# Image/text attention: fourteen slots a group, second scores issued first, values one chunk a slot

## The chip, the cores and the metric

The kernel runs on one core of one Trainium2 chip. The metric is the device time of one execution in microseconds, as the median of the runs shown. The program is one launch that computes eight layers one after the other; the change touches one of them, the image/text attention.

## The reference, cut to what matters

The residual stream x has 4 batches of 256 tokens with 256 channels. The stage below adds an attention of these tokens to a context of 1601 positions a batch: the first 257 are image positions, the other 1344 text. Each kind has its own keys, values and softmax, and the two results are added.

```python
def _L2_xattn_ref(x, context, q_w, ...):          # NH = 16 heads of HD = 16
    ctx_img, ctx_txt = context[:, :257], context[:, 257:]
    q = rms_norm(linear(x, q_w, q_b), norm_q_w).reshape(B, L, NH, HD)
    k = rms_norm(linear(ctx_txt, k_w, k_b), norm_k_w)...      # text
    v = linear(ctx_txt, v_w, v_b)...
    k_img = rms_norm(linear(ctx_img, k_img_w, k_img_b), norm_k_img_w)...
    v_img = linear(ctx_img, v_img_w, v_img_b)...
    out = attention(q, k, v) + attention(q, k_img, v_img)     # softmax(q k / 4) v
    return linear(out, o_w, o_b)

x = x + _L2_xattn_ref(_layernorm(x), ctx_2048, ...)
```

## The kernel before, in words

The function `image_text` (from L1399) does this stage. The host has put the text positions first, so the context is 1344 text columns and then 257 image columns; in chunks of 128 that makes 13 chunks, of which chunk 10 (`mixed`) holds both kinds and chunk 12 has 65 columns. A group is one batch and four heads, so there are 16 groups, four a batch. A head's keys and queries lie on 32 partitions (16 channels, and two more columns that carry the two softmax shifts), so four heads fill the 128 rows of TensorE's array.

Each group is worked on three times:

- First scores, `maxima` (matmul L1572): queries stationary, keys streamed, for the maxima of text and image alone. VectorE reduces them (L1578 text, L1581 image with its sign turned, L1583 over the text pieces). A step takes one query tile of 128 (of two), one of four stretches in `SEGS` (512, 512, 320 and 257 columns) and two heads: 16 steps.
- Second scores, `weights` (L1618): keys stationary, the 256 queries streamed, one pair of chunks and two heads a step: 14 steps, the last two with one chunk. ScalarE takes the exponential into `pt` (L1624).
- Values, `values` (L1639): four heads' matmuls for each chunk, accumulated in one PSUM bank. The mixed chunk counts twice, so there are 14 sets.

All engines but SyncE follow an order written out by hand (`manual_schedule`). Time is cut into slots, `LEN` = 16 for a group. In a slot the loop at the end calls `maxima` for the next group and `weights` for this one, which issue their matmuls at once, and then runs the phases: early, mid (the reductions and exponentials just made), late, pe. Values of a whole pair of chunks come in the pe phase of every second slot from slot 3 on. Slots 14 and 15 have no second scores. First scores of a slot use one half of the array's rows and second scores the other half (`hp`), and the halves swap from slot to slot.

Both kinds of scores draw their PSUM buffer from one ring of three (`ps_sc`, two banks each). Projections, transposes and the output share a ring of one bank (`ps_tr`), and the accumulator is a ring of one (`ps_acc`).

The keys, values and queries of the next batch are produced meanwhile by `produce_keys` and `produce_queries`: a projection (L1527, L1483), one slot later the bias addition on VectorE (L1534, L1489), the square on ScalarE (L1464), the root (VectorE L121, then POOL's power L122), the value copy on POOL (L1538) and the scaling (L1542), then four transposes (L1550), and the copy out of PSUM by `evac`, which alternates between VectorE (L96) and ScalarE (L98). They are placed at `SLOTS` = (2, 5, 8, 11, 15) of three groups of the batch before, those of batch 0 in a prologue of 30 slots. The context comes by one DMA a batch from SyncE's queue (L177), into a single buffer. `finish` copies a group's accumulator (L1651), transposes it (L1656), divides by the sums (L1665 to L1670), and for a batch's last group adds the output projection (L1686, L1699) to x (L181).

Of the kernel before, what the change touches and what calls it, by code (L numbers as in the profile page):

```python
# [18 lines left out]
P = 128  # L19
# [33 lines left out]
def kernel(ctx: ExitStack, tc: tile.TileContext, A, out: bass.AP):  # L53
# [1345 lines left out]
    def image_text(xT):  # L1399
# [4 lines left out]
        half = TXT - mixed * P  # L1404
        G4 = NH2 // 4
        VW = HD2 + 1
        SEGS = [(0, 512), (512, 512), (1024, TXT - 1024), (TXT, IMG)]
        LEN = 16
        groups = [(b, g) for b in range(B) for g in range(G4)]
        ET = mybir.EngineType  # L1410
        with (
# [46 lines left out]
            def heads(ap):  # L1458
                return ap.rearrange("p (h d) -> p h d", h=NH2)

            def rms(src, n):
                sq = pool.tile([P, D], F32, tag="sq", name="sq", bufs=1)
                ss = small([P, 1], "ss1")
                nc.scalar.activation(sq[:n], src, AF.Square, accum_out=ss[:n])  # L1464
                rs = small([P, 1], "rs1")
                rsqrt(rs[:n], ss[:n], 1.0 / D, 1e-6, n, 1)
                return rs

            def fetch(b):
                state[b] = dict(  # L1470
                    ctxT=load_ctxT(b),
                    KT=pool.tile([P, G4, NCTX], F32, tag="KT", name="KT"),
                    QT=pool.tile([P, G4, S], F32, tag="QT0", name="QT0"),
                )

            def produce_queries(b, tt, t, bank):
                Q = qpads[b % 2]
                v = {}

                def project():  # L1480
                    v["ps"] = bank()
                    for c in range(NC_):
                        nc.tensor.matmul(  # L1483
                            v["ps"][:, :D], xtok(xT, b * 2 + tt, c), wq[:, c, :], start=(c == 0), stop=(c == NC_ - 1)
                        )

                def norm():
                    v["kb"] = pool.tile([P, D], F32, tag="kb", name="kb")
                    nc.vector.tensor_tensor(v["kb"], v["ps"][:, :D], qp[:, 0, :], ALU.add)  # L1489
                    v["rs"] = rms(v["kb"], P)  # L1490
                    nc.gpsimd.memset(Q[:, tt, :, HD2 : HD2 + 2], 0.0)

                def scale():
                    nc.vector.scalar_tensor_tensor(
                        Q[:, tt, :, 0:HD2], heads(v["kb"]), v["rs"], heads(qp[:, 1, :]), ALU.mult, ALU.mult
                    )

                def transpose():
                    v["tr"] = ps_tr().rearrange("p (g t) -> p g t", g=G4)
                    for g in range(G4):  # L1500
                        nc.tensor.transpose(
                            v["tr"][:, g, :], Q[:, tt, g * 4 : g * 4 + 4, :].rearrange("p h d -> p (h d)"), ident
                        )

                def out():
                    evac(state[b]["QT"][:, :, tt * P : (tt + 1) * P], v["tr"])

                begin(t, project, norm, scale, transpose, out)

            def begin(t, project, norm, scale, transpose, out):  # L1510
                at(t, "pe", project)
                at(t + 1, "early", norm)
                at(t + 1, "late", scale)
                at(t + 2, "pe", transpose)
                at(t + 3, "early", out)

            def produce_keys(b, k, t, bank):
                o, n = ch[k]
# [13 lines left out]
                def norm():  # L1532
                    v["kv"] = pool.tile([P, 2 * D], F32, tag="kv", name="kv")
                    nc.vector.tensor_tensor(v["kv"][:n], v["ps"][:n], kvp[:n, kind, 0 : 2 * D], ALU.add)  # L1534
                    v["rs"] = rms(v["kv"][:n, 0:D], n)
                    for lo, hi, place in [[(0, n, k)], [(0, half, k), (half, n, nch)], [(0, n, k)]][kind]:
                        vk = vbufs[b % 2][lo:hi, place, 0 : NH2 * VW].rearrange("p (h d) -> p h d", h=NH2)
                        nc.gpsimd.tensor_copy(vk[:, :, 0:HD2], heads(v["kv"][lo:hi, D : 2 * D]))  # L1538

                def scale():  # L1540
                    v["kp"] = kpads[(k % 2, 2, 3 + k % 2)[kind]]
# [11 lines left out]
                        )  # L1553

                def out():
                    evac(state[b]["KT"][:, :, o : o + n], v["tr"][:, :, :n])

                begin(t, project, norm, scale, transpose, out)

            def maxima(i, m):  # L1560

                b, g = groups[i]
                KT, QT, Q = state[b]["KT"], state[b]["QT"], qpads[b % 2]
                tt, s, hp = m // 8, m // 2 % 4, 1 - m % 2
                o, n = SEGS[s]
                if m % 8 == 0:
                    state["mx", tt] = small([P, 4, 3], f"mx{tt}", 2)
                mx = state["mx", tt]
                st = ps_sc()
                for j in range(2):  # L1570
                    r = slice(64 * hp + 32 * j, 64 * hp + 32 * j + 32)
                    nc.tensor.matmul(  # L1572
                        st[:, j, :n], QT[r, g, tt * P : (tt + 1) * P], KT[r, g, o : o + n], start=True, stop=True
                    )

                def rest():
                    if s < 3:
                        nc.vector.tensor_reduce(mx[:, 2 * hp : 2 * hp + 2, s], st[:, :, :n], AX.X, ALU.max)  # L1578
                    else:
                        h = g * 4 + 2 * hp  # L1580
                        nc.vector.tensor_reduce(Q[:, tt, h : h + 2, HD2 + 1], st[:, :, :n], AX.X, ALU.max, negate=True)  # L1581
                    if m % 8 == 7:
                        nc.vector.tensor_reduce(Q[:, tt, g * 4 : g * 4 + 4, HD2], mx, AX.X, ALU.max, negate=True)  # L1583

                return rest

            def queries(i, t):
# [11 lines left out]

                def out():  # L1600
                    state["QT", i] = pool.tile([P, S], F32, tag="QT1", name="QT1")
                    evac(state["QT", i], v["tr"][:, 0:S])

                at(t, "pe", transpose)
                at(t + 1, "early", out)
# [19 lines left out]

                return rest

            def values(i, c):
                b, g = groups[i]
                if c == 0:  # L1630
                    state["acc"] = ps_acc().rearrange("p (k t) -> p k t", k=2)
                acc, V, pt = state["acc"], vbufs[b % 2], state.pop(("pt", i, c))
                for q, (o, n) in enumerate(pairs[c]):
                    k = 2 * c + q
                    kind = (k >= mixed) + (k > mixed)
                    for a, place in [[(0, k)], [(0, k), (1, nch)], [(1, k)]][kind]:
                        for j in range(4):
                            h = g * 4 + j
                            nc.tensor.matmul(  # L1639
                                acc[32 * j : 32 * j + 32, a, :], V[:n, place, h * VW : h * VW + 32], pt[:n, j, q, :],  # L1640
                                start=(k == 0), stop=(k == nch - 1), skip_group_check=True,
                            )

            def finish(i, t):

# [27 lines left out]
                    )  # L1673

                at(t, "early", copy)
                at(t + 3, "pe", transpose)
                at(t + 4, "early", divide)
                if g < G4 - 1:
                    return

# [26 lines left out]
                        nc.gpsimd.tensor_tensor(X[j], X[j], qp[:, 2, :], ALU.add)  # L1707
                        residual(j, v["ps"][:, tt * D : (tt + 1) * D])

                at(t + 6, "pe", turn)  # L1710
                at(t + 7, "early", turned)
                at(t + 9, "pe", project)
                at(t + 10, "early", add)

            first = -30
            SLOTS = (2, 5, 8, 11, 15)
            for b in range(B):
                t0 = LEN * G4 * (b - 1) if b else first
                at(t0 - 2 if b else t0, "early", lambda b=b: fetch(b))
                for k in range(nch + 2):  # L1720
                    t = t0 + (k // 5 * LEN + SLOTS[k % 5] if b else k)
                    bank = (lambda: ps_sc()[:, 0, :]) if b == 0 else ps_tr
                    if k < 2:
                        produce_queries(b, k, t, bank)
                    else:
                        produce_keys(b, k - 2, t, bank)
            n = len(groups)
            for i in range(n):
                queries(i, LEN * i - 2)
                finish(i, LEN * (i + 1))  # L1730
            for t in range(first, LEN * n + 11):
                rest = []
                i, m = divmod(t + 2 + LEN, LEN)
                if 0 <= i < n:
                    rest.append(maxima(i, m))
                i, k = divmod(t, LEN)
                if 0 <= i < n:
                    if k < 2 * len(pairs):
                        rest.append(weights(i, k))
                    if k >= 3 and k % 2:  # L1740
                        at(t, "pe", lambda i=i, c=(k - 3) // 2: values(i, c))
                for phase in ("early", "mid", "late", "pe"):
                    for f in rest if phase == "mid" else todo.pop((t, phase), ()):
                        f()
            if todo:
# [616 lines left out]
```

## Time and profile before

| what | value |
| --- | --- |
| median of three runs | 3859.56 us (3857.51 to 3865.17) |
| the profiled execution | 3858.06 us |
| its span | 3856.3 us |
| TensorE busy in the span | 3603.5 us, 93% |
| VectorE, ScalarE, POOL busy | 2611.3, 1688.0, 1310.3 us |
| second scores L1618 | 1664 matmul passes, 235.7 us busy |
| first scores L1572 | 1024 matmul passes, 229.0 us busy |
| exponentials L1624 | 224, mean 960 ns |
| text reductions L1578 | 192, mean 1089 ns |

The profile is one execution. TensorE's rows count passes: an fp32 matmul appears as two passes, each with its own load of stationary weights (PEld). Lines of the timeline merge instructions of one group: start, length until the last of them ends, engine, line, operation, out and in, the count, and in brackets the idle time of that engine before, with what ended it. The chain of work is followed back from the last instruction; its lines give start, length and what ran. Ends of matmuls are modelled, so starts are the surer times.

### The profile page before, as it was taken

The numbers are of one execution on the slowest core, as the hardware profiler recorded it, in microseconds if no ns is written. First come the engines' busy times: TensorE is split into PE (matmuls) and PEld (weight loads), VectorE is DVE, ScalarE is ACT, GpSimd is POOL, SyncE is SP. The second block draws the span as 40 slices with busy tenths as digits, with TensorE's granted clock in tenths as the row PEclk, the third lists the DMA queues.
The fourth block names the chain that finished last, engine by engine and source line by source line (L and its number), as shares of the span: only waits on it lengthen the run. The fifth ranks groups of instructions, "written<-read, shape, count | busy, mean of one in ns | idle before, by whom it ended". The sixth has DMA issues, their size and how long they took to land.

```text
span 3856.3 us, 63026 instructions
## 1 busy us (share of the span) xinstructions
PE 3603.5 (93%) x23397; PEld 2157.0 (56%) x23397; DVE 2611.3 (68%) x5142; ACT 1688.0 (44%) x4956; POOL 1310.3 (34%) x2091
## 2 busy tenths in 40 slices
PE   8887969999999999999899999987999999999998
PEld 4556944555565555555544454553555556556655
DVE  7884857777777777777665655525767767667664
ACT  4443635444454544444134444422433444444432
POOL 2332534454454444544310101012333333333422
PEclk9987979999999999999989999988999999999999
DMA  7326342222122222220100000033111111211104
GB/s 241 100 67 238 79 150 60 65 71 72 55 60 66 65 81 55 56 54 8 56 18 18 1 18 1 1 132 130 41 55 42 55 32 38 55 38 37 30 3 132
DMA packets 173715, 248.50 MB, mean 64 GB/s; under 512 B 21581, under 2 KB 134881, under 8 KB 169825
## 3 DMA queue, kind: packets, MB, share of 16 engines
q1 hardware_dynamic: 167025, 233.00, 19.5%
q0 software_dynamic: 6384, 11.47, 1.4%
q8 instruction: 186, 3.05, 0.3%
q14 instruction: 120, 0.98, 0.1%
HBM read 199.39 MB, written 45.03 MB: 63 GB/s over the span
## 4 chain that ended last, share of the span: by engine, by line
PE 64%; DVE 18%; POOL 7%; issue 5%; ACT 3%; DMA 3%; SPq 1%; POOLq 0%; DVEq 0%; ACTq 0%
PE acc L1322 15%; PE sc L1242 13%; PE tr L1111 5%; PE sc L1618 4%; DVE PT L1296 4%; PE sc L1572 3%; PE tr L1185 3%; PE acc L1639 3%; POOL pe L1291 3%; PE acc L884 2%; PE tr L1527 2%; PE tr L1335 2%; POOL t L1158 2%; DVE ms L1250 2%; ACT pe L1251 2%
## 5 line engine op out<-in xcount | busy, mean ns | idle before, releaser
L1251 ACT ACTIVATE pe<-sc,ms 128x480 f32<-128x480 f32 (+1 forms) x1024 | 644.0, 632 | 940.2 <-DVE ms L1250 922.9
L1322 PE MATMUL acc<-PT,V 128*128 128x256 f32 (+1 forms) x3584 | 898.4, 391 | 7.7 <-ACT OT L1329 7.2
L1242 PE MATMUL sc<-KT,QT 128*32 128x480 f32 (+5 forms) x8192 | 887.7, 535 | 14.2 <-ACT pe L1251 6.3
L1291 POOL TENSOR_SCALAR pe<-pe,fac 128x480 f32<-128x480 f32 (+1 forms) x1024 | 655.3, 660 | 613.4 <-ACT pe L1251 282.3
L1322 PEld LDWEIGHTS acc<-PT,V 128*128 128x128 f32 (+1 forms) x3584 | 643.2, 190 | 352.2 <-issue 182.1
L1250 DVE TENSOR_REDUCE ms<-sc 128x1 f32<-128x480 f32 (+1 forms) x1024 | 607.5, 615 | 173.3 <-PE sc L1242 147.2
L1296 DVE STREAM_TRANSPOSE PT<-pe 128x1920 f32<-128x1920 f32 (+1 forms) x256 | 519.5, 2030 | 0.0
L122 POOL TENSOR_TENSOR rs<-rsq_t,mhalf 128x2 f32<-128x2 f32 (+2 forms) x248 | 160.1, 646 | 863.8 <-DVE rsq_t L121 804.7
L1242 PEld LDWEIGHTS sc<-KT,QT 128*32 128x32 f32 x8192 | 218.1, 109 | 408.1 <-issue 309.2
L1111 PE MATMUL tr<-w,cx 128*128 128x256 f32 (+1 forms) x1264 | 303.5, 382 | 1.3 <-ACT nk L1127 1.3
L1624 ACT ACTIVATE pt<-sc 128x1024 f32<-128x1024 f32 (+1 forms) x224 | 214.1, 960 | 201.2 <-PE sc L1618 192.9
L1578 DVE TENSOR_REDUCE mx<-sc 128x2 f32<-128x1024 f32 (+1 forms) x192 | 207.2, 1089 | 114.8 <-PE sc L1572 65.5
L1618 PE MATMUL sc<-QT,KT 32*128 32x256 f32 (+1 forms) x1664 | 235.7, 405 | 21.2 <-DVE mx L1578 14.5
L1111 PEld LDWEIGHTS tr<-w,cx 128*128 128x128 f32 (+1 forms) x1264 | 226.7, 187 | 31.6 <-ACT nk L1127 2.0
L1572 PE MATMUL sc<-KT,QT 32*128 32x512 f32 (+2 forms) x1024 | 229.0, 553 | 0.7 <-DVE mx L1578 0.7
L1251 ACT ACTIVATION_READ_ACCUMULATOR pe<-sc,ms 128x1 f32 x1024 | 199.9, 195 | 0.0
L1618 PEld LDWEIGHTS sc<-QT,KT 32*128 32x128 f32 (+1 forms) x1664 | 136.5, 182 | 79.1 <-DVE mx L1578 51.2
L122 POOL TENSOR_TENSOR rsq<-rsq_t,mhalf 128x4 f32<-128x4 f32 x64 | 65.0, 1016 | 326.4 <-DVE rsq_t L121 326.4
L1119 ACT ACTIVATE sq<-tr 128x128 f32<-128x128 f32 (+1 forms) x348 | 97.1, 279 | 169.2 <-PE tr L1111 162.7
L121 DVE TENSOR_SCALAR rsq_t<-ss 128x2 f32<-128x2 f32 (+2 forms) x248 | 45.7, 185 | 172.1 <-ACT sq L1119 134.8
L1185 PE MATMUL tr<-w,xlnT 128*128 128x512 f32 x256 | 126.1, 618 | 4.4 <-DMA w<-in_l1a_wkv 3.2
L1572 PEld LDWEIGHTS sc<-KT,QT 32*128 32x128 f32 x1024 | 84.3, 190 | 76.6 <-issue 42.2
(430 smaller groups left out, 4849.1 us busy)
## 6 DMA issues: line engine op xcount, KB each, us to landing
cx<-in_ctxT SPq DMA_DIRECT2D x144, 256.0 KB, 3.1
tab<-rope SPq DMA_DIRECT2D x112, 256.0 KB, 2.7
w<-in_l0f_w SPq DMA_DIRECT2D x8, 2048.0 KB, 17.0
ctxT<-in_ctxT SPq DMA_DIRECT2D x7, 1601.0 KB, 6.4
w<-in_l2f_w SPq DMA_DIRECT2D x8, 1088.0 KB, 15.6
w<-in_l1a_wq SPq DMA_DIRECT2D x16, 512.0 KB
wo<-in_l1a_wo SPq DMA_DIRECT2D x16, 512.0 KB, 6.4
w<-in_l3a_wq SPq DMA_DIRECT2D x16, 512.0 KB, 7.1
```

What stands on the lines that cost most here:

```text
L122: nc.gpsimd.tensor_tensor(dst, t[:n, :k], mhalf[:n, :k], ALU.pow)
L1111: nc.tensor.matmul(v["ps"][:n, i, :], lhs, st["wkv"][:, c, :], start=(c == 0), stop=(c == NC_ - 1))
L1185: nc.tensor.matmul(v["ps"], xtok(xT, b * 2 + tt, c), state[u]["wq"][:, c, :], start=(c == 0), stop=(c == NC_ - 1))
L1242: nc.tensor.matmul(sc[32 * r : 32 * r + 32, 0 : lens[r]], st["QT"][:, tt, o : o + 32], st["KT"][:, r, 0 : lens[r]], start=True, stop=True,)
L1250: nc.vector.tensor_reduce(top, sc, AX.X, ALU.max, negate=True)
L1251: nc.scalar.activation(w, sc, AF.Exp, bias=top, accum_out=s)
L1291: nc.gpsimd.tensor_scalar(w, w, v["fac"][:, g * 4 + a : g * 4 + a + 1], 1.0, ALU.mult, ALU.mult)
L1296: nc.vector.transpose(state[steps[i]][:, :, g * P : (g + 1) * P].rearrange("p k (a t) -> p a k t", a=4), pes[g].rearrange("p a (k i) -> p ...
L1322: nc.tensor.matmul(v["ps"][:, 0 : 2 * P], V[:n, k, :], PT[:n, k, :], start=(k == 0), stop=(k == nch - 1))
L1572: nc.tensor.matmul(st[:, j, :n], QT[r, g, tt * P : (tt + 1) * P], KT[r, g, o : o + n], start=True, stop=True)
L1618: nc.tensor.matmul(st[:n, j, q, :], KT[r, g, o : o + n], QT[r, :], start=True, stop=True)
L1624: nc.scalar.activation(pt[:n, 2 * hp : 2 * hp + 2, :m], st[:n, :, :m], AF.Exp)
```

## The change

- `LEN` becomes 14. `FIRST` replaces `SEGS`: first scores are made in seven stretches and two halves of heads. The first stretch is the image part of query tile 0 (257 columns); the text of tile 0 followed by text and image of tile 1 is cut into six stretches of 491 (the last 490) columns. One stretch holds the end of tile 0's text and the start of tile 1's, with two matmuls a head and two reductions; one holds text and image.
- In a slot `weights` is called ahead of `maxima`.
- `SETS` lists the 14 sets of values; one set runs in a phase of its own in each of slots 3 to 16, so the last three lie in the next group's slots. `finish` moves with it.
- In production the square, the root and the scaling are spread over two slots; the copies of keys and queries out of PSUM go to VectorE only from batch 1 on, and those of each group's queries always.
- Keys are placed at `SLOTS` over three groups, image chunks first; the queries of a batch lie in the last group of two batches before. The context is asked for four slots ahead of its batch's production instead of two. The prologue has 29 slots.

```diff
-        SEGS = [(0, 512), (512, 512), (1024, TXT - 1024), (TXT, IMG)]
-        LEN = 16
+        LEN = 14
+        step = -(-(TXT + NCTX) // (LEN // 2 - 1))
+        FIRST = [[(0, TXT, IMG)]]
+        for lo in range(0, TXT + NCTX, step):
+            hi = min(lo + step, TXT + NCTX)
+            cuts = [(0, lo, min(hi, TXT) - lo), (1, max(lo, TXT) - TXT, hi - max(lo, TXT))]
+            FIRST.append([c for c in cuts if c[2] > 0])
+        SETS = []
+        for k in range(nch):
+            SETS += [(k, 0, k), (k, 1, nch)] if k == mixed else [(k, int(k > mixed), k)]
...
-            def begin(t, project, norm, scale, transpose, out):
+            def begin(t, project, norm, square, root, scale, transpose, out):
                 at(t, "pe", project)
                 at(t + 1, "early", norm)
-                at(t + 1, "late", scale)
-                at(t + 2, "pe", transpose)
-                at(t + 3, "early", out)
+                at(t + 1, "late", square)
+                at(t + 2, "early", root)
+                at(t + 2, "late", scale)
+                at(t + 3, "pe", transpose)
+                at(t + 4, "early", out)
...
-                    evac(state[b]["KT"][:, :, o : o + n], v["tr"][:, :, :n])
+                    evac(state[b]["KT"][:, :, o : o + n], v["tr"][:, :, :n], "v" if b else "av")
...
             def maxima(i, m):
-                tt, s, hp = m // 8, m // 2 % 4, 1 - m % 2
+                s, hp = m // 2, 1 - m % 2
...
+                for tt, o, n in FIRST[s]:
+                    for j in range(2):
+                        r = slice(64 * hp + 32 * j, 64 * hp + 32 * j + 32)
+                        nc.tensor.matmul(
+                            st[:, j, c : c + n], QT[r, g, tt * P : (tt + 1) * P], KT[r, g, o : o + n],
+                            start=True, stop=True,
+                        )
...
-            def values(i, c):
+            def values(i, x):
+                k, a, place = SETS[x]
...
-                at(t + 3, "pe", transpose)
-                at(t + 4, "early", divide)
+                at(t + 1, "pe", transpose)
+                at(t + 2, "early", divide)
...
-            first = -30
-            SLOTS = (2, 5, 8, 11, 15)
+            SLOTS = (2, 6, 8, 10, 14, 16, 20, 22, 24, 28, 30, 34, 36)
+            ORDER = [*range(mixed, nch), *range(mixed)]
+            first = -29
...
+                tq = (t0 - LEN, t0 - LEN + 6) if b else (t0, t0 + 1)
+                at(t0 - 4 if b else t0, "early", lambda b=b: fetch(b))
+                for i, k in enumerate(ORDER):
+                    produce_keys(b, k, t0 + (SLOTS[i] if b else 2 + i), bank)
...
-                finish(i, LEN * (i + 1))
+                finish(i, LEN * (i + 1) + 3)
+                for x in range(len(SETS)):
+                    at(LEN * i + 3 + x, "values", lambda i=i, x=x: values(i, x))
...
+                if 0 <= i < n and k < 2 * len(pairs):
+                    rest.append(weights(i, k))
                 i, m = divmod(t + 2 + LEN, LEN)
                 if 0 <= i < n:
                     rest.append(maxima(i, m))
-                    if k >= 3 and k % 2:
-                        at(t, "pe", lambda i=i, c=(k - 3) // 2: values(i, c))
-                for phase in ("early", "mid", "late", "pe"):
+                for phase in ("early", "mid", "late", "values", "pe"):
```

## The prediction

> **What bounds the kernel now.** I read the chain of waits first, then the stretches, the waits, and the timeline of one group. The page has TensorE (PE) busy for 93% of the span. The image/text stage runs from about 1890 to 2533 us. These lines of its chain mark groups: the 24 values matmuls (x24, two passes for each fp32 matmul) are slot 15 of a group.
>
> ```profile
> 2438.14 1.92 PE tr L1699 x8
> ...
> 2446.94 1.43 PE acc L1639 x24
> ...
> 2468.32 1.24 DVE mx L1578
> 2469.60 1.13 PE sc L1618 x8
> ...
> 2477.61 1.43 PE acc L1639 x24
> ...
> 2508.28 1.43 PE acc L1639 x24
> ```
>
> A group that produces no keys takes 30.67 us (2446.94 to 2477.61 to 2508.28). Between its matmuls stands a VectorE (DVE) reduction: PE waits for it. The same marker in the busier batches stands at 1990.85, 2032.05, 2073.22, 2106.34 and 2145.22: 41.2 us for a group with five keys. Each of the first three batches takes 154.0 us (462 us from 1953.7, the first second score, to 2415.8).
>
> ```profile
> core 0: us, PE busy (x) PEld busy (x) DVE busy (x) ACT busy (x) POOL busy (x), PEclk, DMA share, GB/s
> ...
> 2261.00:2415.00 154.00, 148.71 (x1296) 77.29 (x1291) 92.54 (x150) 67.54 (x101) 18.68 (x38) 1.00 0.00 1
> 2415.00:2509.00 94.00, 89.01 (x878) 49.16 (x874) 51.61 (x73) 42.89 (x47) 0.00 (x0) 1.00 0.01 1
> ```
>
> DVE is busy 60% of a batch, ScalarE (ACT) 44%, POOL 12%; the granted clock is 1.00 and DMA idle. So the stage has no second full engine; it has PE work and PE waits. Where they lie, one pair of slots shows:
>
> ```profile
> 2462.62 0.70 PE L1572 MATMUL sc<-KT,QT 32*128 32x512 f32 x2
> 2462.64 0.70 PE L1618 MATMUL sc<-QT,KT 32*128 32x256 f32 x4
> 2463.16 0.59 PE L1572 MATMUL sc<-KT,QT 32*128 32x512 f32 x2
> 2463.17 0.60 PE L1618 MATMUL sc<-QT,KT 32*128 32x256 f32 x4
> 2463.60 1.02 PE L1572 MATMUL sc<-KT,QT 32*128 32x512 f32 x4
> 2463.80 2.36 DVE L1578 TENSOR_REDUCE mx<-sc 128x2 f32<-128x1024 f32 x2 [2.35 <-PE sc L1618]
> 2463.95 1.02 ACT L1624 ACTIVATE pt<-sc 128x1024 f32<-128x1024 f32 x1 [1.19 <-PE sc L1618]
> 2465.08 1.13 PE L1618 MATMUL sc<-QT,KT 32*128 32x256 f32 x8 [0.45 <-DVE mx L1578]
> 2466.14 1.07 PE L1639 MATMUL acc<-pt,vbuf 128*32 128x256 f32 x16
> 2467.14 0.70 PE L1572 MATMUL sc<-KT,QT 32*128 32x512 f32 x2
> ```
>
> First scores (L1572) and second scores (L1618) use opposite halves of the array's rows, so they start together. The next second scores need the buffer that DVE is reading: 2462.62 to 2465.08, 2.46 us, of which 0.96 is their work. The pair ends with second scores alone (1.06) and the values of two chunks (1.00): 4.52 us.
>
> **Durations used.** From those rows: a stretch of two passes streams 0.86 us (512 columns, or two times 256), plus 0.10 before it and 0.10 after it where the array's tiling changes. So scores of one slot 1.06, values of one chunk 0.10+0.43+0.10 = 0.63 (two chunks took 1.00). From the first second-score matmul to its exponential: 1.32 (2462.63 to 2463.95) or 1.18 (2465.08 to 2466.26), mean 1.25; exponential 1.02; to the matmul it releases 0.05 (2512.85 to 2512.90 in the last group).
>
> **The change, part by part.**
>
> *Order and ring.* With second scores first and three buffers, second scores reuse what first scores of two slots ago left: DVE has a full slot more and drops out. First scores reuse the buffer of the previous slot's second scores, so they wait for ACT: 1.25+1.02+0.05 = 2.32 us from second scores to the next first scores. Then come first scores (0.10 + 0.82 for 491 columns), 0.10 and values 0.63, 1.65 together. Two slots take 2.32+1.65 = 3.97, about 2.0 a slot, where PE's own work is 1.69. So each slot keeps a wait of 0.3 us, now for ACT. Behind the waiting first scores PE's queue holds the slot's values, transposes and the next second scores, and for those ACT waits in turn; the loop is therefore counted whole.
>
> *Fourteen slots and equal stretches.* First scores keep 3202 columns a group and half of rows and 32 matmuls, but lie in 12 slots of 491 columns beside 512 of second scores, and two of 257 beside 256. The two slots without second scores vanish. A group without keys: 12 x 2.0 = 24.0; two short slots of 0.63+0.63 and 0.15 wait, 2.8; the two query transposes 0.4 and the output's four 0.6 (four took 0.59, 2457.47 to 2458.06), 1.0, half of it inside the ACT wait: 27.3 us, against 30.67. Values of one chunk a slot double the tiling changes; that is in the 0.63. The cut at the end of a query tile adds two reductions a group, 2 x 0.09 us (1024 elements take 1.22, 640 take 0.82, so 0.10 is fixed), beside PE. Values' later slots only shift the end.
>
> *Production.* A key costs PE 1.91 (1.72 stream and changes) plus 0.62 for its transposes, 2.5; the 0.3 waits of the two slots it sits in hide 0.6: 1.9. Before it cost (41.2-30.67)/5 = 2.1. Its PSUM copy-outs move to DVE in later batches (0.69, before half on ACT at 0.58). DVE then does, per two slots with one key, 2 x 1.2 + 0.69 + 0.15 + 0.54 + 0.69 = 4.5 us, PE 2.5 + 3.4 = 5.9: hidden; without that cover it would cost some 0.7 a key. Squares (ACT 0.61) go behind the exponential, scaled roots a slot later, POOL's power (0.54) and value copy (0.40) with them; POOL is 12% busy, and nothing waits at its head. A batch: 4 x 27.3 + 13 x 1.9 + two queries 2.1 (projection 1.05 and transposes 0.6 each, less 0.6) + output projection 1.9 (turn 0.62, project 1.92, less 0.6) = 138. Against 154.0: -16 x 3 = -48.
>
> *Groups 12 to 14*: 3 x 27.3 + 1.9 = 83.8, before 93.9 (2414.35 to 2508.28): -10. *Group 15* has second scores and values only. Before, two slots' second scores ran side by side:
>
> ```profile
> 2512.90 1.13 PE L1618 MATMUL sc<-QT,KT 32*128 32x256 f32 x8 [0.32 <-ACT pt L1624]
> ...
> 2515.55 1.16 PE L1618 MATMUL sc<-QT,KT 32*128 32x256 f32 x16
> ```
>
> Now values stand between: 12 x 1.69 + 2 x 1.26 + 3 values slots at the end is 25 us, before some 18: +7. *Prologue*: key slots took 3.0 us (bias additions at 1907.58, 1910.28, 1913.58), a chain DVE 0.68, ACT 0.61, DVE 0.15, POOL 0.54, DVE 0.59 inside one slot. Split over two slots, PE's 2.5 binds: ten slots x 0.45, and one slot fewer: -6. *Moved loads*: the four context loads (SP queue, 6.4 us to land) are asked for at the latest four slots and 8 us ahead, with nothing else in SP's queue; the buffer is free 20 slots before. No cost; uncovered it would be 6 us each.
>
> **Sum**: -48 -10 +7 -6 = -57 us. The profiled execution took 3858.06 us (span 3856.3), 1.5 under the median 3859.56. 3858.06 - 57 = 3801, plus 1.5: 3802.5.
>
> **A rule against it.** The sum needs first scores to start beside second scores that stand ahead of them in PE's queue with eight passes. The row above shows it: 16 passes take 1.16 us, 8 take 1.13. The second eight belong to the other half of rows and come later in the program. The Trainium skill's "TensorE: Matmul & The Clock Gate", section "The mechanism", says that matmuls keep program order in start and end, and only weight loads go ahead. By it, first scores would start with the last second-score pass, 0.65 us late (0.10 + 3 x 0.215 = 0.75 in, less the 0.10 load): a slot 1.06 - 0.22 + 0.82 + 0.63 = 2.3. Then a group is 12 x 2.3 + 3.0 + 1.0 = 31.6, a batch 126.4 + 13 x 2.5 + 5.9 (queries and output unhidden) = 165, and the stage +33 +3 +7 -6 = +37. I take the row.
>
> **Rivals.**
> 1. *First scores start late* (slower). One mechanism, at PE's queue, priced by the rule: 3858 + 37 + 1.5 = 3897. With a delay d, 39 slots that follow a projection pay d, the other 141 pay d - 0.3: the gain of 57 is gone at d = 0.55. Against it: the last group, and the pair above, where second scores start 0.02 after first scores that have a pass outstanding. Chance 0.08.
> 2. *Smaller gain: a longer ACT or DVE loop.* ACT has copies and squares in its one queue; DVE, between 60% and 76% of a slot pair, may reach a reduction late. If each of 180 slots loses 0.15, -57 becomes -30: 3829. For it: the new wait is real. Against: ACT is 44% busy. Chance 0.11.
> 3. *Nothing moves*: another wait refills what is saved, 3860. The chain runs through these matmuls without a gap, so I give it 0.03.
>
> The forecast has 0.78, with 3789 to 3820: the ends are 0.07 us a slot less wait over 180 slots, and 0.1 more.
>
> **How the numbers follow.** What a measurement can tell from no change is about 0.2%, 8 us. Faster: 0.78 + 0.11 = 0.89; same 0.03; slower 0.08. The range 3789 to 3833 takes the forecast and most of rival 2.
>
> **What would show it.** Markers of groups without keys 27 us apart, of batches 138; first scores waiting for ACT exponentials 0.3 us, DVE waits at second scores gone; first and second scores starting within 0.03 us where neither waits; stage end near 2476. Wrong if first scores start after second scores end, if the x8 values rows are followed by gaps over 0.2, or if batches stay over 150.

## The result, and the profile after

The changed kernel takes **3791.88 us** (median of 6 runs, 3789.63 to 3795.2) against 3859.03 for the kernel before (6 runs beside it). The ratio is 0.9824, with a 95% interval of 0.9811 to 0.9836. The forecast was 3802.5, so the sign, the path and the place were right, and the gain of 67 us is 10 us more than predicted. The profiled execution took 3789.63 us, its span is 3787.9: 68.4 less than before.

The page's first line gives the shares. TensorE (PE) is now busy for 94% of the span instead of 93%, with 44 us less busy time for the same 23397 instructions. In a batch, at a granted clock of 1.00 in both, it is busy for 136.89 us instead of 148.71, because more of them lie side by side.

```profile
PE 3559.4 (94%) x23397; PEld 2124.8 (56%) x23397; DVE 2623.3 (69%) x5204; ACT 1675.6 (44%) x4926; POOL 1315.1 (35%) x2091
```

The stretches of the stage show where the time went. The columns are those of the rows shown of before; the rows are the prologue, a batch, the next batch, and groups 12 to 14.

```profile
core 0: us, PE busy (x) PEld busy (x) DVE busy (x) ACT busy (x) POOL busy (x), PEclk, DMA share, GB/s
...
1888.00:1945.00 57.00, 51.47 (x228) 25.45 (x229) 43.60 (x96) 12.98 (x43) 18.21 (x36) 0.95 0.09 30
...
2088.00:2225.00 137.00, 136.89 (x1286) 69.44 (x1287) 96.54 (x171) 62.45 (x91) 15.36 (x33) 1.00 0.04 13
2225.00:2361.00 136.00, 135.89 (x1300) 68.66 (x1300) 94.27 (x161) 62.80 (x89) 17.67 (x34) 1.00 0.01 2
2361.00:2433.00 72.00, 72.00 (x765) 36.03 (x758) 47.00 (x75) 36.70 (x40) 0.00 (x0) 1.00 0.01 1
```

In a batch PE was idle for 5 us of 154; now for 0.1 of 137. The other engines do what they did, in less time (DVE 96.5 us, 92.5 before: it now has the copies that ScalarE shared).

The chain of waits gives the period. A key's projection at the same place of two batches stands 136.5 us apart from the next, and one slot's values (eight passes) two groups apart in a batch without production stand 55.4 us apart: two groups and an output projection.

```profile
2117.34 1.91 PE tr L1551 x4
...
2253.87 1.91 PE tr L1551 x4
...
2344.07 0.64 PE acc L1674 x8
...
2399.45 0.64 PE acc L1674 x8
```

Where the second scores waited for VectorE before, 85.8 us in all for the two reductions (loads and matmuls together), the trace of after lists almost nothing for them. First the lines of before, then those of after (microseconds, times):

```profile
  DVE mx L1578: 65.7, 85
  DVE qpad L1581: 20.1, 36
```

```profile
  DVE mx L1617: 0.7, 2
  ACT pt L1661: 0.2, 1
```

The timeline of two slots of a group without keys is the counterpart of the pair shown of before:

```profile
2352.95 1.02 ACT L1661 ACTIVATE pt<-sc 128x1024 f32<-128x1024 f32 x1 [1.17 <-PE sc L1603]
...
2353.43 0.92 PE L1655 MATMUL sc<-QT,KT 32*128 32x256 f32 x6
2354.03 0.68 PE L1603 MATMUL sc<-KT,QT 32*128 32x491 f32 x2
2354.18 0.38 PE L1655 MATMUL sc<-QT,KT 32*128 32x256 f32 x2
2354.55 0.58 PE L1603 MATMUL sc<-KT,QT 32*128 32x491 f32 x2
2354.61 1.02 ACT L1661 ACTIVATE pt<-sc 128x1024 f32<-128x1024 f32 x1 [0.63 <-PE sc L1655]
...
2355.05 0.64 PE L1674 MATMUL acc<-pt,vbuf 128*32 128x256 f32 x8
...
2355.62 0.48 PE L1655 MATMUL sc<-QT,KT 32*128 32x256 f32 x2
...
2355.69 0.68 PE L1603 MATMUL sc<-KT,QT 32*128 32x491 f32 x2
...
2355.94 0.60 PE L1655 MATMUL sc<-QT,KT 32*128 32x256 f32 x4
...
2356.37 0.38 PE L1655 MATMUL sc<-QT,KT 32*128 32x256 f32 x2
...
2356.71 0.64 PE L1674 MATMUL acc<-pt,vbuf 65*32 65x256 f32 x8
...
2357.28 0.30 PEld L1655 LDWEIGHTS sc<-QT,KT 32*128 32x128 f32 x4 [0.41 <-issue]
```

Read it from the exponential at 2352.95: it ends at 2353.97, and the first scores (L1603), whose buffer it frees, start at 2354.03, 0.60 after the second scores (L1655). In the next slot the exponential that frees their buffer (2354.61) ends at 2355.63, 0.01 after the second scores started, and the first scores start 0.07 after them. The pair takes 3.85 us (2353.43 to 2357.28), against 4.52.

The wait for ScalarE that takes the place of the one for VectorE is real. The starts of all full slots from 2344 to 2432, which have no keys, put the first scores mostly by turns 0.44 to 0.68 and 0.03 to 0.29 us behind the second scores, 0.32 in the mean. In a stretch with keys (2225 to 2300) it is 0.03 or 0.04 in 20 of 23 full slots. No list of waits shows this as idle time: PE streams the second scores through the other half of the rows meanwhile.

The account by stage, worked out from the starts of matmuls in both traces. The prologue runs from the first query projection to the first group's query transposes (L1595 before, L1632 after), groups from one group's query transposes to the next, and the last part to the start of the last pass of the last output projection:

| us | before | after | difference | predicted |
| --- | --- | --- | --- | --- |
| prologue | 63.4 | 53.6 | -9.8 | -6 |
| batches 0 to 2 | 464.8 | 408.5 | -56.3 | -48 |
| groups 12 to 14 | 92.9 | 81.6 | -11.3 | -10 |
| group 15 | 23.0 | 32.5 | +9.5 | +7 |
| stage | 644.1 | 576.2 | -67.9 | -57 |

The rest of the kernel took 3212.2 us before and 3211.6 after.

### The profile page after: what moved, and what is told of

Same layout as the page of the kernel before. It is cut to its first block, busy times and chain, and to the rows that moved or that the text cites. A ratio compares the mean times of both kernels' runs of the same rounds, so it can differ in the third digit from the quotient of the medians.

```text
span 3787.9 us, 63077 instructions
## 1 busy us (share of the span) xinstructions
PE 3559.4 (94%) x23397; PEld 2124.8 (56%) x23397; DVE 2623.3 (69%) x5204; ACT 1675.6 (44%) x4926; POOL 1315.1 (35%) x2091
## 4 chain that ended last, share of the span: by engine, by line
PE 65%; DVE 16%; POOL 7%; issue 5%; ACT 3%; DMA 3%; SPq 1%; POOLq 0%; DVEq 0%; ACTq 0%
PE acc L1322 15%; PE sc L1242 13%; PE tr L1111 5%; PE sc L1655 4%; DVE PT L1296 4%; PE acc L1674 3%; PE tr L1185 3%; POOL pe L1291 3%; PE sc L1603 3%; PE acc L884 3%; PE tr L1551 2%; POOL t L1158 2%; DVE ms L1250 2%; PE tr L1335 2%; ACT pe L1251 2%
## 5 line engine op out<-in xcount | busy, mean ns | idle before, releaser
L1242 PEld LDWEIGHTS sc<-KT,QT 128*32 128x32 f32 x8192 | 218.1, 109 | 408.5 <-issue 309.2
L1617 DVE TENSOR_REDUCE mx<-sc 128x2 f32<-128x982 f32 (+2 forms) x224 | 211.5, 957 | 94.8 <-PE sc L1603 61.6
L1655 PE MATMUL sc<-QT,KT 32*128 32x256 f32 (+1 forms) x1664 | 240.4, 403 | 0.0
L1603 PE MATMUL sc<-KT,QT 32*128 32x491 f32 (+4 forms) x1024 | 233.7, 551 | 0.0
L1655 PEld LDWEIGHTS sc<-QT,KT 32*128 32x128 f32 (+1 forms) x1664 | 139.0, 182 | 92.5 <-issue 72.5
L1674 PE MATMUL acc<-pt,vbuf 128*32 128x256 f32 (+1 forms) x1792 | 142.5, 391 | 0.0
```

What stands on the lines that cost most here:

```text
L1242: nc.tensor.matmul(sc[32 * r : 32 * r + 32, 0 : lens[r]], st["QT"][:, tt, o : o + 32], st["KT"][:, r, 0 : lens[r]], start=True, stop=True,)
L1603: nc.tensor.matmul(st[:, j, c : c + n], QT[r, g, tt * P : (tt + 1) * P], KT[r, g, o : o + n], start=True, stop=True,)
L1655: nc.tensor.matmul(st[:n, j, q, :], KT[r, g, o : o + n], QT[r, :], start=True, stop=True)
L1674: nc.tensor.matmul(acc[32 * j : 32 * j + 32, a, :], V[:n, place, h * VW : h * VW + 32], pt[:n, j, q, :], start=(k == 0), stop=(k == nch - ...
```

## The experiments

Each kernel is the changed one with one edit, except the second, which is the kernel before with one part of the change. Ratios are to the kernel before, run on the same chip beside it; "stage" is the total of the account above, 576.2 for the change.

**First scores issued ahead again.** In the slot loop the two blocks change places:

```diff
+                i, m = divmod(t + 2 + LEN, LEN)
+                if 0 <= i < n:
+                    rest.append(maxima(i, m))
                 if 0 <= i < n and k < 2 * len(pairs):
                     rest.append(weights(i, k))
-                i, m = divmod(t + 2 + LEN, LEN)
-                if 0 <= i < n:
-                    rest.append(maxima(i, m))
```

> The changed kernel (3791.9 us) with first scores issued ahead of second scores again in every slot; all else as changed. Theory A (the gain is the sum of shorter PE work and a wait that is only exchanged, reduction for exponential, of nearly the same length): second scores wait again for the reduction of the slot before, 1.13 + 1.18 + 0.05 = 2.36 us from first scores, against 2.25 from second scores over the exponential; 0.1 us a slot in the 141 slots without a projection, +14: about 3806. Rival B (the order is the gain): the 0.45 us a slot that the old kernel waited comes back in 180 slots, +50 or more: 3840 and up. Rival C (order does nothing): 3792.

Measured 3813.45 us, 0.9874 (0.9854 to 0.9895); stage 596.0. The order is worth 20 us in the new frame. The sign is that of the first theory, whose 3806 lies 7 us below. The wait for VectorE is back, in the timeline of this kernel:

```profile
2374.16 1.18 DVE L1617 TENSOR_REDUCE mx<-sc 128x2 f32<-128x982 f32 x1 [0.90 <-PE sc L1603]
...
2374.95 0.68 PE L1603 MATMUL sc<-KT,QT 32*128 32x491 f32 x2
2375.39 0.49 PE L1655 MATMUL sc<-QT,KT 32*128 32x256 f32 x2
```

Second scores start at 2375.39, 0.05 after the reduction ends (2375.34) and 0.44 after the first scores. It costs about the same in every group after the first: 28.0 us against 26.8 in one without keys, 39.4 against 38.2 in one with. A reduction of 982 columns takes 1.18, and the slot leaves it nearly enough room.

**Second scores issued ahead, in the kernel before.** The same exchange, the other way round, in sixteen slots with values in pairs:

```diff
-                i, m = divmod(t + 2 + LEN, LEN)
-                if 0 <= i < n:
-                    rest.append(maxima(i, m))
                 i, k = divmod(t, LEN)
                 if 0 <= i < n:
...
                     if k >= 3 and k % 2:
                         at(t, "pe", lambda i=i, c=(k - 3) // 2: values(i, c))
+                i, m = divmod(t + 2 + LEN, LEN)
+                if 0 <= i < n:
+                    rest.append(maxima(i, m))
```

> The kernel before (3859.0 us) with this one edit: second scores issued ahead of first scores. Sixteen slots and values of two chunks every second slot stay. Theory A: a pair of slots is 2.25 + 0.93 + 0.10 + 1.00 = 4.28 us beside 512 columns (was 4.52), but about 4.0 beside 320 (was 3.80) and 3.9 beside 257 (was 3.56), because the second first-score stretch now waits for an exponential of full length: it nets to nothing, 3851 to 3867. Rival B (the order is the gain): 0.3 us a slot, 3800 to 3825.

Measured 3858.02 us, 0.9987 (0.9975 to 1.0); stage 640.1, 4 us less than before. In the old frame the order alone is worth next to nothing. The waits of this kernel show why: over about two groups (2440 to 2500) PE's loads for first scores now wait 8.9 us for the exponential, where those for second scores waited 8.8 for the reduction before (2446.94 to 2508.28, reductions of the text alone).

```profile
PEld sc L1572 <- ACT pt L1624: 8.9, 11, 1.1
```

**Values of two chunks in every second slot.**

```diff
-                    at(LEN * i + 3 + x, "values", lambda i=i, x=x: values(i, x))
+                    at(LEN * i + 3 + (x | 1), "values", lambda i=i, x=x: values(i, x))
```

> The changed kernel with values of two sets in every second slot instead of one set in each, so seven changes of tiling a group fewer in each direction. Theory A: values between the slots fill the wait for the exponential; in pairs, a pair of slots takes 2.25 + 0.92 + 0.10 + 1.00 = 4.27 us against 3.85, +0.4 in some 51 pairs without keys, -0.2 in the 39 with keys, where PE has no wait: +10 to +20, about 3805. Rival D (the doubled tiling changes are a cost that the change only carries along): -0.27 us for each of 90 pairs, 3768.

Measured 3820.07 us, 0.9898 (0.9875 to 0.9921); stage 605.3. This loses 29 us, although it saves tiling changes, and loses in groups with keys and without (29.6 against 26.8). The expected size, 10 to 20, was too small. The timeline shows a slot without values between second and first scores of neighbouring slots:

```profile
2394.66 1.03 PE L1655 MATMUL sc<-QT,KT 32*128 32x256 f32 x8
...
2395.95 1.09 PE L1603 MATMUL sc<-KT,QT 32*128 32x491 f32 x4 [0.27 <-ACT pt L1661]
...
2396.98 0.42 PE L1674 MATMUL acc<-pt,vbuf 128*32 128x256 f32 x4
```

First scores start 1.29 us after the second scores started and 0.27 after PE last streamed anything: they wait for an exponential that has not had the 0.63 us of a slot's values to run beside. So values in every slot are cover for the exponential; that is what the doubled tiling changes buy. In the last group, where no first scores wait, the pairs win: 25.4 against 32.5, of which 0.9 is a higher granted clock in the last output projection.

**Both kinds of scores in the same half of the rows.**

```diff
-                s, hp = m // 2, 1 - m % 2
+                s, hp = m // 2, m % 2
```

> The changed kernel with first scores on the same half of the array's rows as the slot's second scores, so that they can't run side by side: it prices the delay of rival 1 of the prediction. First scores then start 0.86 us after second scores. By that rival's formula, 39 slots x 0.86 + 141 x (0.86 - 0.3) = +112: about 3904. If running side by side were worth little (PE bound by something other than the streams), it stays near 3792.

Measured 3916.17 us, 1.0145 (1.0121 to 1.0169): slower than before, and 12 us above the expected 3904; stage 700.0. This is the prediction's first rival made real. The timeline has first scores behind all eight passes of second scores, and a slot of 2.46 us:

```profile
2430.31 1.13 PE L1655 MATMUL sc<-QT,KT 32*128 32x256 f32 x8
...
2431.28 0.99 PE L1603 MATMUL sc<-KT,QT 32*128 32x491 f32 x4
...
2432.20 0.64 PE L1674 MATMUL acc<-pt,vbuf 128*32 128x256 f32 x8
```

The overlap of the two kinds is thus worth 124 us of stage, nearly twice the whole gain.

**A shorter exponential.** It runs on half of the queries' columns, and the other half of the weights is a constant:

```diff
-                    nc.scalar.activation(pt[:n, 2 * hp : 2 * hp + 2, :m], st[:n, :, :m], AF.Exp)
+                    nc.scalar.activation(pt[:n, 2 * hp : 2 * hp + 2, :m, 0:P], st[:n, :, :m, 0:P], AF.Exp)
```

> The changed kernel with each exponential over half of its columns (the first 128 of 256 queries; the other half of the weights is a constant, so this work is left out). It takes 0.59 us instead of 1.02. Theory A (first scores wait for the exponential of the slot before): the pair of slots falls from 3.85 us to 1.82 + 1.65 = 3.47, near PE's own 3.38: 0.19 us a slot in 141 slots, -20 to -30, about 3766. Rival E (the reduction or PE alone sets the slot): 3789 to 3792.

Measured 3771.09 us, 0.9774 (0.9759 to 0.9789); stage 552.8. Its lines lie six or seven lower. The exponential takes 0.60, and both slots of a pair have first scores early:

```profile
2339.50 0.60 ACT L1668 ACTIVATE pt<-sc 128x512 f32<-128x512 f32 x1 [1.32 <-PE sc L1661]
...
2339.89 0.48 PE L1661 MATMUL sc<-QT,KT 32*128 32x256 f32 x2
2340.15 0.68 PE L1609 MATMUL sc<-KT,QT 32*128 32x491 f32 x2
...
2341.74 0.48 PE L1661 MATMUL sc<-QT,KT 32*128 32x256 f32 x2
2341.78 0.68 PE L1609 MATMUL sc<-KT,QT 32*128 32x491 f32 x2
...
2343.38 0.48 PE L1661 MATMUL sc<-QT,KT 32*128 32x256 f32 x2
```

The pair takes 3.49 (2339.89 to 2343.38) instead of 3.85, so the exponential is on the path. That is so most of all where no keys are produced: a group without production takes 24.3 us instead of 26.6, one with five keys 37.6 instead of 38.2. The last slot of the lines, without a wait, takes 1.64: PE's own work.

**Shorter reductions.** The maxima are taken over half of the columns:

```diff
-                        nc.vector.tensor_reduce(top, sc, AX.X, ALU.max, negate=negate)
+                        nc.vector.tensor_reduce(top, sc[:, :, 0 : sc.shape[2] // 2], AX.X, ALU.max, negate=negate)
```

> The changed kernel with each reduction of first scores over half of its columns (the maxima are of half of the columns: work left out), 0.64 us instead of 1.18. Theory A: the reduction has a slot to spare, so batches stay; only the prologue, where first scores alone wait for it, gains some 3 us: 3786 to 3791. Rival E (VectorE sets the slot): -0.27 us a slot or more, 3745.

Measured 3780.68 us, 0.9799 (0.9784 to 0.9814), 5 us below the expected range; stage 567.8. The starts say where. The prologue is 3.6 us shorter and group 0 another 4.1 (32.7 against 36.8); the other groups of batch 0, batches 1 and 2 and groups 12 to 14 are the same to 0.1 us. So VectorE is off the path from group 1 on.

What group 0 gains is in the main the granted clock's, not VectorE's. The rows are group 0 of the change and, after the gap, of this kernel; the columns are those of the stretches above.

```profile
1941.60:1978.50 36.90, 35.59 (x281) 18.41 (x280) 24.39 (x40) 14.46 (x21) 4.09 (x9) 0.85 0.00 1
```

```profile
1941.10:1973.90 32.80, 31.68 (x281) 15.99 (x280) 17.58 (x42) 14.35 (x21) 4.15 (x9) 1.00 0.00 1
```

The same 281 passes keep PE busy for 35.59 us at 0.85 and for 31.68 at 1.00: 3.9 of the 4.1 us. Why the clock stays at 1.00 here was not tested. The end of the prologue has the higher clock too (0.79 from 1930 to 1945 in the change, 1.00 here), so how much of the 3.6 us the reductions alone are worth stays open. That PE waits for them there, the changed kernel's chain shows:

```profile
1931.75 2.31 DVE mx L1617 x4
...
1934.13 1.09 DVE mx L1617
```

**A key's chain inside one slot again.** Square and root follow the bias addition at once, and the scaling comes in the same slot's late phase; the second kernel keeps the transposes a slot earlier in the prologue.

```diff
-                at(t + 1, "late", square)
-                at(t + 2, "early", root)
-                at(t + 2, "late", scale)
-                at(t + 3, "pe", transpose)
-                at(t + 4, "early", out)
+                late = t >= LEN * 0
+                at(t + 1, "early", square, root)
+                at(t + 1, "late", scale)
+                at(t + 2 + late, "pe", transpose)
+                at(t + 3 + late, "early", out)
```

The first kernel of the two has the transposes at t + 3 everywhere:

> The changed kernel with a key's square, root and scaling in one slot again, as before the change; transposes keep their place. VectorE then stands waiting for ScalarE and POOL inside the slot, about 1.2 us a key (0.6 and 0.7 in the old prologue). Theory A: VectorE's spare time covers most of it in the batches (4.5 + 1.2 = 5.7 of 5.9 us), 0 to +5; the prologue's ten slots grow from 2.15 to about 2.9, +7: 3796 to 3804. Rival F (the split is a main part of the gain): 0.5 us a key and more on top, 3815.

It took 3845.76 us, 0.9966 (0.9952 to 0.9979), and missed by 42. Its prologue is 95.9 us: there the transposes follow the scaling of a later key into the same buffer, so they wait a whole cycle for it, and batch 0 gets keys of other chunks. Its batches cost 3.3 to 4.2 us each. The second kernel, with the transposes in step:

> The same edit as the run of the chain in one slot, mended: there, in the prologue, a key's transposes followed the scaling of the key after next into the same buffer, so its prologue (95.9 us) priced another order. Here the prologue's transposes and copies also move one slot ahead, as before the change, so that each key's own scaling is what they wait for. Batches should repeat what that run showed, +3 to +4 us each (0.3 us a key). Theory A: prologue from 53.6 to 60 to 64 us (63.4 before the change), stage +17 to +21: about 3810. If the split is not what shortened the prologue: prologue 54 to 57, 3803.

It took 3819.67 us, 0.9881 (0.9864 to 0.9898), 10 above the expected 3810; stage 598.5, which is 22 over the change. The prologue is 12.6 longer (66.2), the batches 3.3 to 3.6 each; the one that produces no queries has 3.3, or 0.25 us for each of 13 keys. So the split over two slots is worth 13 us where keys alone make the slot, and something in the batches too, where I had taken it for hidden.

**The last group's values in pairs, and the copies.** Three kernels change what should matter little. The first takes pairs for group 15 alone, the second lets the key copies of batches 1 to 3 alternate between VectorE and ScalarE as before, the third has the pairs, and in the prologue puts the copies on ScalarE:

```diff
-                    at(LEN * i + 3 + x, "values", lambda i=i, x=x: values(i, x))
+                    at(LEN * i + 3 + (x | 1 if i == n - 1 else x), "values", lambda i=i, x=x: values(i, x))
...
-                    evac(state[b]["KT"][:, :, o : o + n], v["tr"][:, :, :n], "v" if b else "av")
+                    evac(state[b]["KT"][:, :, o : o + n], v["tr"][:, :, :n])
...
-                    evac(state[b]["QT"][:, :, tt * P : (tt + 1) * P], v["tr"], "v" if b else "av")
+                    evac(state[b]["QT"][:, :, tt * P : (tt + 1) * P], v["tr"], "v" if b > 1 else "a")
...
-                    evac(state[b]["KT"][:, :, o : o + n], v["tr"][:, :, :n], "v" if b else "av")
+                    evac(state[b]["KT"][:, :, o : o + n], v["tr"][:, :, :n], "v" if b else "a")
```

> The changed kernel, but the last group, which has no first scores beside it, takes its values two sets in every second slot, so second scores of two slots run side by side as they did before. From the last query transposes to the last output projection the kernel before took 23.0 us, the changed one 32.5. Theory A: 6 to 8 us come back: 3784 to 3786, faster than both. If ScalarE's exponentials (14 x 1.0 us) or the tail set the end of this group: 3790 or more.

> The changed kernel with copies of keys out of PSUM shared by VectorE and ScalarE in all batches again (alternating). Theory A: VectorE does 4.5 us of work in the 5.9 us of two slots with a key, so its 0.69 us copies are hidden, and slots with keys don't wait for ScalarE: -2 to +5, 3790 to 3797. Rival: VectorE is late in these slots, and relief by half of 39 copies gives 0.3 us each, -6 and more: 3786.

> A version meant to be faster: the last group's values in pairs (-4.9 us in its own run), and the copies of the prologue's keys and queries all on ScalarE, because with halved reductions the prologue and the first group gained 3.5 + 4.1 us: there VectorE is what is late. Taken off VectorE while first scores wait for it: three copies of keys and two of queries, some 3.2 us. Theory A: 3781 to 3785, prologue and first group 2 to 4 us shorter. If VectorE's lateness there is from the reductions alone: 3786 to 3788.

The pairs: 3788.63 us, 0.9817 (0.9803 to 0.983), stage 570.8. Group 15 takes 27.6 us instead of 32.5, both with the last output projection at half the granted clock (see below): 4.9 come back where 6 to 8 were expected. The timelines of group 15 of the change and, after the gap, of the kernel with pairs:

```profile
2434.85 1.13 PE L1655 MATMUL sc<-QT,KT 32*128 32x256 f32 x8
2435.91 0.64 PE L1674 MATMUL acc<-pt,vbuf 128*32 128x256 f32 x8
2436.48 1.13 PE L1655 MATMUL sc<-QT,KT 32*128 32x256 f32 x8
```

```profile
2442.72 1.16 PE L1655 MATMUL sc<-QT,KT 32*128 32x256 f32 x16
...
2443.81 1.07 PE L1674 MATMUL acc<-pt,vbuf 128*32 128x256 f32 x16
```

With values between, each slot's second scores stand alone, 1.63 us a slot; in pairs two slots share 1.16, 2.09 for the two (2442.72 to 2444.81).

The shared copies: 3797.11 us, 0.9827 (0.9809 to 0.9845), stage 576.5 against 576.2: nothing, as the prediction had it. The third kernel: 3790.58 us, 0.9812 (0.9798 to 0.9825), beside the change itself once more:

> The changed kernel itself, unedited, beside these three on one chip: the value that they are compared with. 3790 to 3794, ratio to the kernel before 0.982.

which took 3792.87, 0.9819 (0.9805 to 0.9832), stage 576.0. The third kernel's stage is 570.7: 3.4 of the difference lie in group 15 (27.6 against 31.0, its output projection at half clock and the other's at full), 1.0 in the prologue and 0.9 in batch 0. The change's own two profiles differ there by 0.3 and 1.0, so the copies bring at most a microsecond or two. Its 3781 to 3785 were not reached: the medians are 2.3 us apart and the intervals overlap. The larger part of what it rested on was not VectorE's: group 0's 4.1 us were mainly the clock's. No version that does all of the work was shown by its times to beat the change; what the traces show is the last group's 5 us.

## Why the prediction was right, and where 10 us were missed

- **What bounds the stage.** Right: PE's waits at the scores, not another engine. That VectorE drops out and ScalarE takes its place with a smaller wait is shown by the start times, by the shorter exponential (-23 us) and by the shorter reductions (no effect from group 1 on). The 0.3 us a slot that the working gave the new wait are 0.32 by the starts, and production hides them, as said. (The x24 rows that mark the groups are not slot 15's but slot 13's, which has the two sets of the mixed chunk and chunk 11; the period is the same.)
- **The pair of slots, 3.97 us.** It takes 3.85, and two terms are at fault by 0.06 each. One is the mean of 1.25 us from second scores to their exponential. Here it is 1.18 in both slots (2353.43 to 2354.61): the wait is 1.18 + 1.02 + 0.05 = 2.25 instead of 2.32, measured 2.26 to the next first scores at 2355.69. The other is the 0.63 for values: from 2355.69 on, first scores take 1.02 as reckoned (to 2356.71) and values 0.57 (to 2357.28), together 1.59 instead of 1.65. 0.12 less a pair is some 0.7 a group, and a group without production takes 26.6 to 26.8 instead of 27.3.
- **Production, 1.9 a key.** Right in sum: a batch of 136.5 less 4 x 26.8 leaves 29.3 for production, where 13 x 1.9 + 2.1 + 1.9 = 28.7 was taken. The 1.9 has no wait for the chain of a key in it. The run with the chain in one slot shows that this holds because of the split, which is worth 3.3 to 3.6 a batch; no term for the batches gave it a price. The copies moved to VectorE cost nothing, as said.
- **Batches.** With the two, 137.7, 136.5 and 134.3 against 138; the last has no next queries to produce, which the working did not take off. A part of the -56 against -48 is the counting: the 462 us of the prediction began at the first second score, the 464.8 of the account at the query transposes.
- **Prologue, -6.** The size failed at "PE's 2.5 binds". That number carried two tiling changes around the projection; between transposes and projection of the prologue there is none to pay, as the chain shows:

```profile
1907.03 0.44 PE tr L1579 x4
1907.47 1.72 PE sc L1551 x4
1909.19 0.44 PE tr L1579 x4
1909.63 1.72 PE sc L1551 x4
```

  A slot is 2.15 us, not 2.5. From the first key's projection to the thirteenth's it is 27.5 us (1892.15 to 1919.65), before 38.1 (1895.06 to 1933.20): -10.6. The start gives another -2.3, and the tail, from there to the first group's query transposes, takes 3.2 more: there VectorE binds, which the working of the prologue left out. The granted clock is also lower in the tail of both (0.69 from 1935 to 1954 before, 0.79 from 1930 to 1945 after), and once earlier in the kernel before (0.50 from 1894.5 to 1897.9); what that is worth beside VectorE was not measured apart.
- **Group 15, +7.** Right, though the table has +9.5. The profiled execution made its last output projection at a granted clock of 0.51:

```profile
2461.00:2464.50 3.50, 3.45 (x8) 2.53 (x8) 0.00 (x0) 0.00 (x0) 0.00 (x0) 0.51 0.00 0
```

  It took 3.67 us there, 1.99 before (2531.06) at 1.00. To the start of its last pass, where the account ends, that is 3.15 against 1.62. Without this 1.5 the group costs +8.0, and so it does in the second run of the change, at 1.00 in this place (31.0 for the part). The values between the scores are the cause, as reckoned, at 1.63 a slot.
- **The rule against it.** The Trainium skill's "TensorE: Matmul & The Clock Gate", section "The mechanism", says that matmuls keep program order in start and end. The measurement decides otherwise here: first scores start at 2355.69, while six of the eight passes of second scores ahead of them in the program are still to start (2355.94 x4, 2356.37 x2). Where both kinds share the rows, first scores do come last, and the stage costs 124 us more. The rival's working has 94 between the two orders (+37 against -57): it took a delay of 0.65, and in that kernel it is 0.97 (2430.31 to 2431.28).
- **The smaller-gain rival** does not occur: from group 1 on VectorE is never late enough to matter, and the loop through ScalarE costs the 0.3 us a slot that were taken for it, not more.

**Where the gain lies.** Undone one at a time in the new kernel, the order is worth 20 us, values of one chunk a slot 29, and the split of the chain 22, in stage time; the order alone in the old kernel is worth 4. That these sum to 71, near the whole gain, does not make them an account: the order is worth 20 in one frame and 4 in the other, so the parts depend on each other. The fourteen slots with equal stretches were not tried alone, and what they bring by themselves stays open.

## What to carry to other kernels

When one wait is replaced by another, count the new loop whole (matmul, exponential, release) and ask what work stands in it: here the values between the slots are the cover that makes the new wait small. Taken away alone they cost 29 us, and the same reordering in the old frame, with values in pairs, was worth 4 us of 68. Work in opposite halves of the array's rows at once is worth 124 us in this stage; before you move an instruction, see that its neighbour still lies in the other half. Take durations from rows that have the same neighbours as in the new place: the terms that missed were a mean over two different slots, a values time 0.06 too long, and tiling changes that the prologue does not have.

## What the runs showed of the hardware

A wait at the head of PE's queue need not appear as idle time. Where no keys are produced, first scores start 0.44 to 0.68 us late in about every second slot, yet the lists of waits over 2344 to 2427 give them 0.4 us in all; only the starts show it, and the shorter exponential its price, 23 us. And a change of tiling (whole array or parts of it) has a price: a key's projection takes 1.91 us between scores and values, which use parts of the array (32*128 and 128*32 in the lines), and 1.72 in the prologue, where it follows transposes that use the whole array as it does. That makes some 0.1 us on either side, an estimate from these two times.

Last, the granted clock moves single parts of a profile. It was 0.51 for the eight passes of the last output projection in one profile of the change, right after a stage that ran at 1.00, and 1.00 in the other: 3.67 us against 1.99. It was 0.85 over group 0 of the change and 1.00 with the shorter reductions: 35.59 us of PE's time against 31.68 for the same passes. So a short stretch is not compared between single profiles without the clock beside it, and an experiment that shortens one engine's work is read for the clock before the gain is put down to that engine.
